# Turned sums ahead of a unit's own sums, and the last two node blocks side by side, in a two-layer graph network on one Trainium2 core

## The chip, the cores and the metric

One core of a Trainium2 chip runs the whole program. The metric is the device time of one execution in microseconds (us); several runs of the kernel before are given below. Five engines work side by side: PE multiplies matrices, DVE does elementwise vector work, ACT does activation functions and copies, POOL issues the gathers, SP issues most other transfers.

## The reference, cut to what matters

6250 nodes have 160 features each, 200000 edges join them and are sorted by their target node. Two layers follow each other; each sends messages over the edges, sums them by target, mixes the sums, adds the node's own part and normalises:

```
for layer in (0, 1):
    t   = per-node linear mix of x                    # the table that edges read
    w   = silu(edge_scalars @ fc1) @ fc2              # weights of an edge, 192 or 224
    msg = products of w, t[src] and 4 edge attributes # 448 or 640 wide
    agg = segment_sum(msg, dst)                       # by target node
    x   = layernorm(x + mix(agg) + own_mix(x))        # layer 1: silu and gates before the sum
```

Layer 1's table is made of layer 0's result, so no edge of layer 1 can be read before the last node of layer 0 is done.

## The kernel before, in words

Edges go in **tiles** of 128 (1563 of them), two tiles are a **pair** (782), four are a **unit** (391). Nodes go in **blocks** of 128 (49, named b0 to b48). Since edges are sorted, a run of 3 to 12 tiles touches at most 32 neighbouring nodes; such a run is a **group** (284 of them, named g0 to g283; n = 12 tiles at first, 4 tiles from about three quarters of the way on, 3 in the last fifth). `GROUPS`, `READY` (which group must be done before a block may be finished) and the tests on them are lines 37 to 68.

The loop of `windows` (lines 824 to 850) runs over units u, and each step works on several units at once:

- `gather` (line 703) for unit u+4: POOL issues one indirect DMA a tile. A gathered pair lies in one of 8 buffers `g`, so a gather waits for the products of 8 pairs earlier.
- `weights` (line 695, tile `pw`, 3 PSUM banks) for unit u+2 on PE: called W below.
- `hidden` (lines 646 to 677) for unit u+3: PE writes the two PSUM banks `pair0` and `pair1` (H below), ACT applies Silu out of them into `h`. In layer 0 one unit uses both banks, in layer 1 bank u % 2.
- `places` (line 734, tile `sel`) and `products` (line 721, tile `mid`) for the two pairs of unit u+2, all on DVE.
- `aggregate` (line 754, tile `pg`) for the four tiles of unit u on PE: A below. At a group's end ACT copies `pg` into `r` (and `rest` in layer 1).
- `turn` (lines 768 to 783) for the groups that ended in the unit before: PE transposes `r` into columns 256 and up of bank `pair[g % 2]` (T below), and DVE adds it into the sums `sm` and `sr` in SBUF (lines 781, 783), which hold all nodes.
- one step of the block that is being finished (`proceed`, line 816). In layer 0 these are `summed` (S below: PE multiplies `sm` and `sr`, DVE and ACT normalise), `turn` (line 520, n below: two transposes) and `mix` (m below: PE, then ACT writes the row to `table[1]`, the table that layer 1 gathers from). In layer 1 there is only `summed` (lines 558 to 582), which writes the output.
- one step of the own part of a block to come (`prepare`, line 796), in the middle of A: fetch, `self_part`, `self_mix`.

The order of PE's instructions is the order in which the program calls them: `matmul` and `transpose` (lines 137 to 145) pin it. DVE and ACT follow the order that the scheduler of the framework gives them, near the program's. All node work uses one PSUM bank, `pn` (bufs=1). PE's order in one unit of layer 0 is W, H, A, T, block step.

After the last unit, line 855 runs what is left of block steps one block after the other.

Of the kernel before, what the change touches and what calls it, by code (L numbers as in the profile page):

```python
# [16 lines left out]
P = 128  # L17
# [69 lines left out]
def kernel(ctx: ExitStack, tc: tile.TileContext, a, out):  # L87
# [345 lines left out]
    def turned(x, work, tag, bufs):  # L433

        n = x.shape[0]
        p = psum.tile([P, 512], F32, name=tag, bufs=bufs)
        transpose(p[:, 0:n], x[:, 0:P], ident[:n, :n])
        transpose(p[:V, P:P + n], x[:, P:D], ident[:n, :n])
        xt = work.tile([P, 2, P], F32, name="xt")
        nc.scalar.activation(xt[:, 0, :n], p[:, 0:n], AF.Copy)  # L440
        nc.scalar.activation(xt[:V, 1, :n], p[:V, P:P + n], AF.Copy)
        return xt
# [33 lines left out]
    def second_nodes(b, work, clear, name="nx"):  # L476


        n = rows_of(b)
        rows = slice(b * P, b * P + n)  # L480
        st = {}

        def fetch():
            x = st["x"] = work.tile([P, D], F32, name=name, bufs=4 if name == "nx" else 1)
            if b in owned:
                nc.sync.dma_start(x[:n], xown[rows, :])
            else:
                nc.sync.dma_start(x[:n], a["x_main"][:, b, :] if b < NB - 1 else a["x_tail"])

        def self_part():  # L490
            st["xs"] = turned(st["x"][:n], work, "pn", 1)

        def self_mix():
            x = st["x"]
            q = mixed(st["xs"], n, wsc, "pn", 1)
            for k in range(2):
                nc.vector.scalar_tensor_tensor(x[:n], q[:, k, :], own[:n, b, k:k + 1], x[:n],
                                               op0=OP.mult, op1=OP.add)
            return x

        def summed():
            p = psum.tile([P, 512], F32, name="pn", bufs=1)
            q = p[:n, :2 * D].rearrange("p (w d) -> p w d", w=2)
            for c in range(4):
                l = sm[:96, c, rows]
                if c < 2:
                    matmul(q[:, :, 0:S + V], l, rm0[:, c], start=(c == 0), stop=False)
                else:
                    v = S + (c - 1) * V
                    matmul(q[:, :, 0:S], l, rm0[:, c, :, 0:S], start=False, stop=False)  # L510
                    matmul(q[:, :, v:v + V], l, rm0[:, c, :, S:], start=False, stop=False)
            matmul(q[:, :, S + V:D], sr[:64, rows], rr0, start=False, stop=True)
            y = st["x"][:n]
            for k in range(2):
                nc.vector.scalar_tensor_tensor(y, q[:, k, :], gets[:n, b, k:k + 1], y,
                                               op0=OP.mult, op1=OP.add)
            mv = work.tile([P, 8], F32, name="mv")
            normed(y, mv)

        def turn():  # L520
            st["xt"] = turned(st["x"][:n], work, "pn", 1)

        def mix():
            xt = st["xt"]
            p = psum.tile([P, 512], F32, name="pn", bufs=1)
            matmul(p[:n, 0:P], xt[:, 0, :n], who[0][:, :P], start=True, stop=True)
            matmul(p[:n, P:D], xt[:V, 1, :n], who[1][:, :V], start=True, stop=True)
            r = work.tile([P, D], F32, name="nr")
            nc.scalar.activation(r[:n], p[:n, 0:D], AF.Copy, scale=nv[:n, b, 0:1])
            nc.scalar.dma_start(table[1][rows, :], r[:n])  # L530
            nc.scalar.dma_start(xmid[rows, :], st["x"][:n])
            if clear:
                nc.vector.memset(sm[:, :, b * P:b * P + P], 0.0)
                nc.vector.memset(sr[:, b * P:b * P + P], 0.0)

        return [fetch] + [self_part, self_mix] * (b not in owned), [summed, turn, mix]

    def last_nodes(b, work, clear):
        n = rows_of(b)
        rows = slice(b * P, b * P + n)  # L540
        st = {}

        def fetch():
            x = st["x"] = work.tile([P, D], F32, name="nx", bufs=4)
            nc.sync.dma_start(x[:n], xmid[rows, :])

        def self_part():
            st["xs"] = turned(st["x"][:n], work, "pn", 1)

        def self_mix():  # L550
            xt = st["xs"]
            p = psum.tile([P, 512], F32, name="pn", bufs=1)
            matmul(p[:n, 0:160], xt[:, 0, :n], who[0][:, P:], start=True, stop=True)
            matmul(p[:n, 160:192], xt[:V, 1, :n], who[1][:, V:], start=True, stop=True)
            o = st["o"] = work.tile([P, 192], F32, name="no", bufs=4)
            nc.scalar.activation(o[:n], p[:n, 0:192], AF.Copy)

        def summed():
            x, o = st["x"][:n], st["o"][:n]
            p = psum.tile([P, 512], F32, name="pn", bufs=1)  # L560
            q = p[:n, :192]
            matmul(q, sr[:, rows], rr1, start=True, stop=False)
            matmul(q[:, 0:160], sm[:, 0, rows], rm1[:, 0, 0:160], start=False, stop=False)
            for c in (1, 2, 3):
                v = slice(96 if c == 2 else 0, 192)
                matmul(q[:, v], sm[:, c, rows], rm1[:, c, v], start=False, stop=(c == 3))
            nc.vector.tensor_tensor(o, q, o, OP.add)
            f = nv[:n, b, 0:1]
            y = work.tile([P, D], F32, name="nr")
            nc.scalar.activation(y[:n, 0:S], o[:, 0:S], AF.Silu, scale=f)  # L570

            gate = work.tile([P, V], F32, name="gate")
            nc.scalar.activation(gate[:n], o[:, S:96], AF.Tanh, scale=half[:n, b])
            nc.vector.tensor_scalar(gate[:n], gate[:n], 1.0, half[:n, b], op0=OP.add, op1=OP.mult)
            nc.vector.tensor_tensor(
                y[:n, S:D].rearrange("p (c d) -> p c d", c=3),
                o[:, 96:192].rearrange("p (c d) -> p c d", c=3),
                gate[:n, None, :].to_broadcast([n, 3, V]), OP.mult)
            nc.vector.tensor_tensor(x, y[:n], x, OP.add)
            mv = work.tile([P, 8], F32, name="mv")  # L580
            normed(x, mv)
            nc.scalar.dma_start(out[rows, :], x)

        return [fetch, self_part, self_mix], [summed]


    def windows(i, loads, work, inputs_of):
# [208 lines left out]
        def prepare():  # L796

            if early:
                early.pop(0)()
            elif not coming and left and len(prepared) < 2:  # L800
                b = left.pop(0)
                if b in later:
                    later.remove(b)
                first_, then = nodes(b, work, i == 0)
                first_.pop(0)()
                coming.extend(first_)
                coming.append((b, then))
            elif len(coming) > 1:
                coming.pop(0)()
            elif later:  # L810
                early.extend(own_nodes(later.pop(0), work))
                early.pop(0)()
            if len(coming) == 1:
                prepared.append(coming.pop())
# [6 lines left out]
                going.pop(0)()  # L821
            return going or prepared

        for u in range(-4, units + 1):
            before = turned_to
            if i == 0 and ZERO + 4 + u < NB:
                zero(ZERO + 4 + u)
            if u + 4 < units:
                for p in pairs_of(u + 4):
                    gather(p)  # L830
            if 0 <= u + 2 < units:
                weights(pairs_of(u + 2))
            if 0 <= u + 3 < units:
                hidden(u + 3)
            if 0 <= u + 2 < units:
                for p in pairs_of(u + 2):
                    places(p)
                    products(p)
            if u >= 0:
                ended, waiting = waiting, []  # L840
                for t in range(4 * u, min(4 * u + 4, NT)):
                    if t == 4 * u + 2:
                        prepare()
                    aggregate(t)
                    if group_of[t][2]:
                        waiting.append(group_of[t][0])
                for g in ended:
                    turn(g)
                    turned_to = g + 1
                proceed(turned_to if u + 3 > units else before)  # L850
        for g in waiting:
            turn(g)
        while coming or left:
            prepare()
        while proceed(NG):
            pass


    def general(i, loads, work):
# [176 lines left out]
```

## Time and profile before

| what | us |
|---|---|
| runs of the kernel, median (lowest, highest) | 4095.0 (4084.81, 4096.76) |
| the profiled execution: its time, its span | 4098.12, 4096.3 |
| before the first gather | 65.8 |
| gathers of layer 0, first to last | 1989.0 |
| from the last gather of layer 0 to the first of layer 1 | 34.6 |
| gathers of layer 1, first to last | 1968.5 |
| after the last gather | 38.4 |
| busy: PE, DVE, POOL, ACT | 3522.1, 3095.1, 3026.7, 1176.1 |

A line of the timeline reads: start, duration, engine, line of the kernel, operation, written tile `<-` read tiles, shapes, how many such instructions were merged, and in brackets the idle time of the engine before it with what ended it. A line of the waits reads: engine, tile and line, what it waited for, us in total, how often, the longest. In the windows, each engine has its busy time and the number of its instructions, and PEclk is the granted clock of PE as a share of full speed. PE's records come two to a matmul.

### The profile page before, as it was taken

The numbers are of one execution on the slowest core, as the hardware profiler recorded it, in microseconds if no ns is written. First come the engines' busy times: TensorE is split into PE (matmuls) and PEld (weight loads), VectorE is DVE, ScalarE is ACT, GpSimd is POOL, SyncE is SP. The second block draws the span as 40 slices with busy tenths as digits, with TensorE's granted clock in tenths as the row PEclk, the third lists the DMA queues.
The fourth block names the chain that finished last, engine by engine and source line by source line (L and its number), as shares of the span: only waits on it lengthen the run. The fifth ranks groups of instructions, "written<-read, shape, count | busy, mean of one in ns | idle before, by whom it ended". The sixth has DMA issues, their size and how long they took to land. (4 is left out here: it accounts for less than half of the span.)

```text
span 4096.3 us, 108196 instructions
## 1 busy us (share of the span) xinstructions
PE 3522.1 (86%) x37363; PEld 2419.1 (59%) x37363; DVE 3095.1 (76%) x13202; ACT 1176.1 (29%) x4013; POOL 3026.7 (74%) x3232
## 2 busy tenths in 40 slices
PE   7788988889899999999978888888788888888887
PEld 5565666666666666666655555555555555555555
DVE  6676666667777777777757777777778888888887
ACT  2122221222222333333311111122223333444454
POOL 4777777777777777777757777777777777777774
PEclk8899898889899999999978888889989999998998
DMA  4233322222222232333323333333333333333332
GB/s 128 78 84 87 81 75 77 78 76 79 77 79 79 79 82 79 82 84 80 87 71 94 96 95 97 98 96 96 100 97 97 103 100 96 106 100 98 101 103 59
DMA packets 298517, 364.05 MB, mean 89 GB/s; under 512 B 86323, under 2 KB 246204, under 8 KB 297964
## 3 DMA queue, kind: packets, MB, share of 16 engines
q0 software_dynamic: 151056, 257.36, 23.8%
q1 hardware_dynamic: 121740, 85.59, 7.4%
q10 hardware_dynamic: 25168, 14.11, 1.1%
q8 instruction: 300, 4.92, 0.5%
q14 instruction: 253, 2.07, 0.2%
HBM read 338.73 MB, written 18.03 MB: 87 GB/s over the span
## 5 line engine op out<-in xcount | busy, mean ns | idle before, releaser
L703 POOL DMA_INDIRECT g<-table,src x3126 | 3004.9, 961 | 1026.8 <-issue 736.9
L721 DVE TENSOR_TENSOR mid<-g,pw 128x128 f32<-128x128 f32 (+2 forms) x7820 | 1852.8, 299 | 653.0 <-DMA g<-table,src 416.1
L138 PE MATMUL pw<-fc,h 100*128 100x192 f32 (+1 forms) x6252 | 1225.5, 383 | 193.4 <-DVE mid L721 186.4
L138 PE MATMUL pg<-mid,sel 128*32 128x160 f32 (+1 forms) x25008 | 1155.1, 305 | 0.0
L138 PEld LDWEIGHTS pw<-fc,h 100*128 100x128 f32 (+1 forms) x6252 | 895.9, 203 | 369.9 <-issue 315.0
L138 PEld LDWEIGHTS pg<-mid,sel 128*32 128x32 f32 x25008 | 755.3, 116 | 387.7 <-issue 320.7
L734 DVE SCALAR_TENSOR_TENSOR sel<-iota,off,ea 128x128 f32<-128x128 f32 x3126 | 940.5, 341 | 39.4 <-PE pg L138 35.0
L138 PE MATMUL pair<-e,fc 64*100 64x256 f32 (+1 forms) x2348 | 606.2, 454 | 120.2 <-DVE sr L783 113.4
L665 ACT ACTIVATE h<-pair 100x256 f32<-100x256 f32 x782 | 260.7, 381 | 954.6 <-PE pair L138 941.0
L138 PEld LDWEIGHTS pair<-e,fc 64*100 64x100 f32 (+1 forms) x2348 | 239.5, 183 | 351.2 <-issue 193.1
L676 ACT ACTIVATE h<-pair 128x256 f32<-128x256 f32 x392 | 150.5, 384 | 960.5 <-PE pair L138 795.6
L143 PE MATMUL pair<-ident,r 128*96 128x128 f32 (+1 forms) x852 | 225.7, 291 | 27.6 <-ACT h L665 21.7
L138 PE MATMUL pn<-rm,sm 96*128 96x128 f32 (+4 forms) x980 | 192.1, 356 | 51.2 <-DVE sm L781 49.6
L759 ACT ACTIVATE r<-pg 128x96 f32<-128x96 f32 (+1 forms) x568 | 149.5, 263 | 297.8 <-PE pg L138 228.5
L781 DVE TENSOR_TENSOR sm<-pair,sm 96x128 f32 (+1 forms) x568 | 161.9, 285 | 92.1 <-PE pair L143 19.1
L143 PEld LDWEIGHTS pair<-ident,r 128*96 128x96 f32 (+1 forms) x852 | 107.8, 127 | 206.0 <-issue 105.3
L765 ACT ACTIVATE rest<-pg 32x32 f32<-32x32 f32 x1136 | 209.5, 184 | 12.5
L138 PEld LDWEIGHTS pn<-rm,sm 96*128 96x128 f32 (+3 forms) x980 | 176.3, 235 | 59.9 <-DVE sm L781 53.3
L138 PE MATMUL pn<-rr,sr 64*128 64x128 f32 (+2 forms) x196 | 66.1, 426 | 93.4 <-DVE sr L783 89.0
L458 ACT ACT_TABLE_LOAD x97 | 124.5, 1283 | 7.1 <-DVE mv L457 5.4
L138 PEld LDWEIGHTS pair<-fold,rest 128*128 128x128 f32 x568 | 104.0, 226 | 1.1 <-ACT rest L765 1.1
L783 DVE TENSOR_TENSOR sr<-pair,sr 64x32 f32 (+1 forms) x568 | 99.7, 176 | 0.8 <-DVE sm L781 0.6
(137 smaller groups left out, 1313.0 us busy)
## 6 DMA issues: line engine op xcount, KB each, us to landing
g<-table,src POOLq DMA_INDIRECT x3126
e<-in_e SPq DMA_DIRECT2D x781, 64.0 KB
e<-in_e SPq DMA_DIRECT2D x390, 20.0 KB
ea<-in_ea_main SPq DMA_DIRECT2D x63, 96.0 KB
xg<-in_x_main SPq DMA_DIRECT2D x12, 320.0 KB
table<-rg SPq DMA_DIRECT2D x12, 320.0 KB
xmid<-nx ACTq DMA_DIRECT2D x48, 80.0 KB
table<-nr ACTq DMA_DIRECT2D x48, 80.0 KB
```

The source lines that it names most:

```text
L138: r = nc.tensor.matmul(*args, **kw)
L143: r = nc.tensor.transpose(*args)
L458: nc.scalar.activation(mv[:n, 1:2], mv[:n, 1:2], AF.Sqrt, bias=eps[:n])
L665: nc.scalar.activation(h[:100, 2 * P * j:2 * P * j + m], pair[j][:100, :m], AF.Silu)
L676: nc.scalar.activation(h[:kk, c0:c1], p[:kk, c0:c1], AF.Silu, scale=0.125)
L703: nc.gpsimd.indirect_dma_start(out=g[:n, j, :], out_offset=None, in_=table[i][:, :], in_offset=bass.IndirectOffsetOnAxis(ap=of(t)[0], axis=0))
L721: nc.vector.tensor_tensor(parts(mid[:n, :m], V * place, V * step, k), parts(g[:n, :m], c, V, k), parts(q[:n, :m], w, w_step, k), OP.mult)
L734: made["last"] = nc.vector.scalar_tensor_tensor(s[:n, j], iota[:n, None, :].to_broadcast([n, 4, W]), w, e[:, :, None].to_broadcast([n, 4, ...
L759: nc.scalar.activation(r[:, :w], pg[:, :w], AF.Copy)
L765: nc.scalar.activation(rest[g % 3][k, k], pg[k, P:P + V], AF.Copy)
L781: nc.vector.tensor_tensor(sm[:h, :, at], pt[:h, :P].rearrange("p (c w) -> p c w", c=4), sm[:h, :, at], OP.add)
L783: made["last"] = nc.vector.tensor_tensor(sr[:k, at], pt[:k, P:P + W], sr[:k, at], OP.add)
```

## The change

1. `turn` of the groups that ended in the unit before is called between the two pairs of `places` and `products`, that is ahead of `aggregate`. PE's order in a unit becomes W, H, T, A, block step; DVE's becomes first pair, adds, second pair.
2. The block b48 takes its PSUM tiles for node work from `pw` (3 banks) in place of `pn`, and in layer 0 its steps alternate with those of the block before it, after the last unit. The loop has one step less, and the last unit makes no block step.
3. `prepare` fetches a new block while fewer than three are prepared or in hand (four for the last one), in place of two prepared. By the rule of the loops, b48's own part in layer 1 comes at units 382 to 384 and not at 387 to 389; in layer 0 b47 and b48 are fetched at units 381 and 382 and not at 382 and 387.
4. In layer 1's last block an ACT instruction on one column calls Sqrt right after the gate's Tanh; the gate gets a tile of its own for input and output, and `mv` a ninth column for it.

```diff
+        bank = ("pn", 1) if b < NB - 1 else ("pw", 3)
...
-            p = psum.tile([P, 512], F32, name="pn", bufs=1)
+            p = psum.tile([P, 512], F32, name=bank[0], bufs=bank[1])
...
-            st["xt"] = turned(st["x"][:n], work, "pn", 1)
+            st["xt"] = turned(st["x"][:n], work, *bank)
...
+            if b == NB - 1:
+                nc.scalar.activation(mv[:n, 8:9], gates[:n, 0, 0:1], AF.Sqrt, bias=eps[:n], scale=0.0)
...
-            elif not coming and left and len(prepared) < 2:
+            elif not coming and left and len(prepared) + bool(going) < 3 + (left[0] == NB - 1):
...
-        for u in range(-4, units + 1):
+        for u in range(-4, units):
...
-            if 0 <= u + 2 < units:
-                for p in pairs_of(u + 2):
-                    places(p)
-                    products(p)
+            ps = pairs_of(u + 2) if 0 <= u + 2 < units else []
+            for p in ps[:1]:
+                places(p)
+                products(p)
+
+            ended, waiting = waiting, []
+            for g in ended:
+                turn(g)
+                turned_to = g + 1
+            for p in ps[1:]:
+                places(p)
+                products(p)
             if u >= 0:
-                ended, waiting = waiting, []
                 for t in range(4 * u, min(4 * u + 4, NT)):
                     if t == 4 * u + 2:
                         prepare()
                     aggregate(t)
                     if group_of[t][2]:
                         waiting.append(group_of[t][0])
-                for g in ended:
-                    turn(g)
-                    turned_to = g + 1
-                proceed(turned_to if u + 3 > units else before)
+                if u < units - 1:
+                    proceed(turned_to if u + 3 > units else before)
         for g in waiting:
             turn(g)
         while coming or left:
             prepare()
-        while proceed(NG):
-            pass
+
+        chains = [going] + [steps for _, steps in prepared]
+        while any(chains):
+            for steps in chains:
+                if steps:
+                    steps.pop(0)()
```

More of the change, by code (lines that the diff above doesn't have):

```diff
@@ L516, in summed @@
                                                op0=OP.mult, op1=OP.add)
-            mv = work.tile([P, 8], F32, name="mv")
+            mv = work.tile([P, 9], F32, name="mv")
             normed(y, mv)
         def turn():
-            st["xt"] = turned(st["x"][:n], work, "pn", 1)
+            st["xt"] = turned(st["x"][:n], work, *bank)
         def mix():
             xt = st["xt"]
-            p = psum.tile([P, 512], F32, name="pn", bufs=1)
+            p = psum.tile([P, 512], F32, name=bank[0], bufs=bank[1])
             matmul(p[:n, 0:P], xt[:, 0, :n], who[0][:, :P], start=True, stop=True)
@@ L570, in summed @@
             nc.scalar.activation(y[:n, 0:S], o[:, 0:S], AF.Silu, scale=f)
-            gate = work.tile([P, V], F32, name="gate")
-            nc.scalar.activation(gate[:n], o[:, S:96], AF.Tanh, scale=half[:n, b])
-            nc.vector.tensor_scalar(gate[:n], gate[:n], 1.0, half[:n, b], op0=OP.add, op1=OP.mult)
+            gates = work.tile([P, 2, V], F32, name="gate")
+            nc.scalar.activation(gates[:n, 0], o[:, S:96], AF.Tanh, scale=half[:n, b])
+            mv = work.tile([P, 9], F32, name="mv")
+            if b == NB - 1:
+                nc.scalar.activation(mv[:n, 8:9], gates[:n, 0, 0:1], AF.Sqrt, bias=eps[:n], scale=0.0)
+            gate = gates[:, 1]
+            nc.vector.tensor_scalar(gate[:n], gates[:n, 0], 1.0, half[:n, b], op0=OP.add,
+                                    op1=OP.mult)
             nc.vector.tensor_tensor(
@@ L579, in summed @@
             nc.vector.tensor_tensor(x, y[:n], x, OP.add)
-            mv = work.tile([P, 8], F32, name="mv")
             normed(x, mv)
```

## The prediction, before the result was known

> **What bounds the kernel now.** I read the page first, for the span (4096.3) and the costliest group, then POOL's waits.
>
> ```profile
> L703 POOL DMA_INDIRECT g<-table,src x3126 | 3004.9, 961 | 1026.8 <-issue 736.9
> ```
>
> ```profile
> POOL g L703 <- issue: 736.9, 2417, 0.3
> POOL g L703 <- DVE mid L721: 110.3, 361, 0.5
> ...
> POOL g L703 <- DMA nx<-xmid: 34.6, 1, 34.6
> ```
>
> POOL issues 3126 gathers of 961 ns, with 0.3 us between any two whatever is named as releaser; only one idle in the loops is longer, the 34.6 us between the layers. So in both layers POOL never stops, and the span is 65.8 + 1989.0 + 34.6 + 1968.5 + 38.4 = 4096.3. Next to nothing can be gained inside a layer. A gain must come out of the 34.6 and the 38.4, and a loss comes where another engine stops keeping POOL's pace.
>
> So I asked next who is nearest to that pace, by windows and in the timeline of late layer 0 (windows: PE, clock, DMA share, GB/s):
>
> ```profile
> 1746.00:1896.00 150.00, 140.09 (x1524) 0.95 0.30 80
> ```
>
> ```profile
> 1911.35 0.68 PE L138 MATMUL pair<-e,fc 64*100 64x256 f32 x4
> 1911.96 1.27 PE L138 MATMUL pg<-mid,sel 128*32 128x160 f32 x32
> ...
> 1918.49 1.75 PE L138 MATMUL pn<-rm,sm 96*128 96x192 f32 x12 [1.17 <-DVE sm L781]
> ...
> 1922.09 0.68 PE L138 MATMUL pair<-e,fc 64*100 64x256 f32 x4
> 1922.70 1.27 PE L138 MATMUL pg<-mid,sel 128*32 128x160 f32 x32
> 1924.70 0.85 PE L143 MATMUL pair<-ident,r 128*96 128x128 f32 x4 [0.73 <-ACT h L665]
> ```
>
> ACT in the same stretch:
>
> ```profile
> 1912.06 0.66 ACT L665 ACTIVATE h<-pair 100x256 f32<-100x256 f32 x2 [1.71 <-PE pair L138]
> ...
> 1922.70 1.28 ACT L665 ACT_TABLE_LOAD   x1
> 1923.99 0.66 ACT L665 ACTIVATE h<-pair 100x256 f32<-100x256 f32 x2
> ```
>
> PE is busy 140.1 of 150. From one start to the next, W takes 1.50, H 0.61, A 1.21, a T 0.39; a block's S takes 2.10, n 0.27, m 0.75. Late in layer 0 there is one block to four units and 5.33 groups, so four units cost PE 4 x 3.32 + 5.33 x 0.39 + 3.12 = 18.5, and with the waits shown (S for DVE's add 1.17, T for ACT's `h` 0.73) 20.4. POOL issued 118 gathers in those 150 us, 1.271 each: 20.3 for the sixteen of four units. PE has no slack there at all.
>
> **Part 1, T ahead of A, layer 0.** PE's last row shows a wait that matters more after the change: T starts 0.05 after ACT has finished with the bank that H wrote (h ends at 1924.65). T writes the same bank, so it can't pass Silu. Now A (1.21) lies between H and T and hides this. In front of A it is bare. By the rows of 1911: PE is free for T at 1911.96, `h` of the first bank ends at 1912.41 and of the second at 1912.72, so T waits 0.50 or 0.81, mean 0.65. After a summed block ACT first loads a table: at 1922.70 PE is free, T could start at 1924.37 or 1924.70, a wait of 1.85 in the mean. Four units now need 18.5 + 3 x 0.65 + 1.85 = 22.3, without the 1.17 and 0.73. PE becomes the bound by 2.0 in 20.3.
>
> How long: from unit 268 (its W at 1445) to the W of unit 388 (2060) PE has 120 units, all with a T: 120 x 3.32 + 143 turns x 0.39 + 25 blocks x 3.12 = 532, and the waits 95 x 0.65 + 25 x 1.85 = 108: 640 for the 615 now, **+25**. (Before unit 268 there are fewer turns and blocks, and PE stays under POOL's pace.) Queued behind the waiting T are A, the block step and the next W; DVE waits for T with its adds and, in order behind them, the second pair's products; these free the `g` buffers, and after about 13 us of lag POOL waits too.
>
> The clock comes on top. PE waited 1.47 at 1576.68, and the windows view gives 0.50 for 1578.3 to 1585.1: W took 2.93 in place of 1.50. Over the trace's clock records, 16 of 22 idle gaps of 1.8 to 2.0 us were followed by half clock, mostly for 3.4 or 6.8 us. The new 1.85 comes once a block: between 0 and 25 x 0.73 x 3.4 = 62. I take every second block at 2.8 of lost PE time, **+35**, a bit under the nearest rows, since in 6.8 us some of the time is waiting anyway.
>
> The Trainium skill ("TensorE: Matmul & The Clock Gate", "Why this matters for your kernels") sets the limit for dropping the clock at idle gaps of about 3 us between bursts. By it the clock would hold at 1.85 and the 35 would be 0; the rows at 1576 differ, and they decide.
>
> The other side of part 1: S no longer waits for the add, which DVE now does ahead of the second pair. In layer 0 this is in the 640.
>
> **Between the layers.**
>
> ```profile
> 2049.14 3.08 PE L138 MATMUL pn<-rm,sm 96*128 96x192 f32 x12 [3.16 <-DVE sm L781]
> ...
> 2076.47 3.11 PE L138 MATMUL pn<-rm,sm 96*106 96x192 f32 x12 [0.48 <-ACT nr L529]
> ```
>
> The first row is b46's S: 3.16 late, then at half speed (it is in the 615, not in the 640). The second is b48's S, waiting for `pn` until b47's mix has been copied, 7.7 after b47's S ended (2068.8). Side by side it needs b47's transposes (4.35 after S) and the adds of g282 and g283 (about 4.9 after): 2.8 earlier; the loop's end before it is about as long: **-3**, bounds 0 and -5. From there to the first gather of layer 1 at 2089.39 (12.9) the chain is as now. Layer 0 in sum: 25 + 35 - 3 = +57.
>
> **Layer 1 and the tail.** PE's four units there, by the timeline from 3925 to 3962 (each step from its start to the next): W 0.95, H 0.63, A 1.23, T with its gap 0.50, a block 2.83 (S 1.66, own part 0.37 and 0.80), T's wait about 0.45, since only half of the turns meet the bank of H: 17.6 of 20.1; PE stays free. DVE is near its limit:
>
> ```profile
> 4066.52 0.36 DVE L567 TENSOR_TENSOR no<-pn,no 128x192 f32<-128x192 f32 x1 [2.30 <-PE pn L138]
> ...
> 4074.24 0.90 DVE L721 TENSOR_TENSOR mid<-g,pw 64x64 f32<-64x64 f32 x6
> ```
>
> The last gather ends at 4057.89, its product starts at 4074.24: 16.35 behind, where 1.64 is the least in the trace and about 4 the mean two thirds through. DVE's cycle between two blocks is 20.3 (3934.90 to 3955.21), POOL's 20.1; in it `no` waits for PE's S, 63.0 us over 38 blocks, 1.66 each. With the adds ahead of the second pair (1.9 of DVE work, as long as S), that wait goes, DVE has 18.7 for 20.1, and the lag shrinks to about 6: **-10**, bounds 0 (what is saved is lost on T) and -14.7 (all lag). From the last product to b48's S (10.75 now) the chain of turns stays, so nothing more is counted.
>
> **The rest, each at 0.** The bank in layer 1: `pn` was read by 4080.33, b48's S started at 4084.99. The early Sqrt: the table load now runs from 4089.11 to 4090.39, hidden by DVE's steps up to 4090.60; the added call (0.29 by its sibling) lies beside DVE's gate. b48's own part leaves units 387 to 389: 1.3 of PE and 0.8 of ACT beside DVE's products, 0 to -1. The fetches on SP move one to five units forward, with four `nx` buffers; a wait of SP is covered by the three units that `e` is ahead. Moved parts issue the same DMAs as now.
>
> **Sum.** 57 - 10 = +47 on the profiled 4098.1 is 4145; the runs' median is 3.1 below that execution, so **4142**.
>
> **Rivals.** (B) PE is the bound but the clock holds: without the 35, +12, 4107. The 16 of 22 speak against it; that PE would be steadily loaded otherwise, for it. Range 4090 to 4120. (C) **Faster**: PE's bare T is absorbed. The buffers hold 13 us, and if T's mean wait is under about 0.4 (that is 18.5 + 1.6 = 20.1 for four units, POOL's pace) nothing of it reaches POOL. Then the end of layer 0 also loses the 3.16 and its half-speed units (S 1.3, W 1.4, H 0.5, A 1.1 longer than at full clock): -10 with the 2.8, and the tail gives -12: 4073. The rows of 1911 and 1922 speak against it; for it, that `h` could come sooner after H when ACT is idle. (D) DVE's order is the scheduler's, and the adds may stay behind the second pair: the change then doesn't do what it says on DVE, S waits as now, the tail's 10 is lost: 4152 or, on top of B, 4117. I count it into A and B.
>
> **Chances.** A (forecast) 0.50, 4115 to 4180; B 0.33; C 0.17. About 0.3% (12 us) can be told from no change. Slower by more (over 4107): A and half of B, 0.665; within: the other half of B and a little of C, 0.195; faster (under 4083): 0.14. The range 4078 to 4180 leaves out most of C and the top of A, under 0.2.
>
> **What would show it.** Right: POOL's waits for DVE mid grow late in layer 0 and its 1989.0 becomes some 2030 or more; `PE L143 <- ACT h L665` grows from 21.7 to over 150; PEclk late in layer 0 falls under 0.95; `no <- PE pn` nearly goes and the 38.4 falls to about 28. Wrong: the gathers of layer 0 still take 1989 with T waiting (C), or the wait of T is not there at all.

## The result and the profile after

The changed kernel takes 4184.02 us in the median of four runs (4172.53 to 4191.97), the kernel before 4093.91 on the same chip. The ratio is 1.0227, interval 1.0205 to 1.0248: **slower by 90 us, where the forecast was 47**, and 4 us above the forecast's range. The profiled execution took 4183.07 us, span 4181.3.

| part of the span, us | before | after | difference | forecast |
|---|---|---|---|---|
| before the first gather | 65.8 | 66.0 | +0.2 | 0 |
| gathers of layer 0 | 1989.0 | 2075.3 | +86.3 | +60 |
| last gather of layer 0 to first of layer 1 | 34.6 | 45.6 | +11.0 | -3 |
| gathers of layer 1 | 1968.5 | 1962.6 | -5.9 | 0 |
| after the last gather | 38.4 | 31.8 | -6.6 | -10 |

In the kernel after, a line that was 721 is 728, 665 is 672, 734 is 741, 781 is 788, 783 is 790, 567 is 569; 143 and 460 are as before. The costliest group and two of POOL's waits, where POOL never stopped inside a layer before:

```profile
L710 POOL DMA_INDIRECT g<-table,src x3126 | 2999.3, 959 | 1124.0 <-issue 740.2
```

```profile
POOL g L710 <- DVE mid L728: 178.8, 336, 5.0
POOL g L710 <- DMA nx<-xmid: 45.6, 1, 45.6
```

The gathers themselves are as short as before (959 ns for 961), so the time that was added stands in the idle column: 1124.0 us for 1026.8, 97 more. POOL's idle times are no longer 0.3 us each: a wait for the products has 5.0 us for its longest, where 0.5 was the longest before. Now the window that the forecast showed of before (140.09 us of PE's 150, the clock at 0.95), taken of after. The columns are the window, its length, the busy times of PE, PE's weight loads, DVE, ACT and POOL with the number of their instructions, then the clock, the DMA share and the GB/s:

```profile
1746.00:1896.00 150.00, 122.11 (x1235) 88.20 (x1234) 95.70 (x403) 47.71 (x145) 97.67 (x101) 0.91 0.26 70
```

Every engine is less busy than before (PE 122 us for 140, DVE 96 for 116, ACT 48 for 54), and POOL issues 101 gathers for 118. A learner who looks for the busiest engine finds none. PE is nevertheless what ends last, and its waits say why:

```profile
PE pair L143 <- ACT h L672: 225.6, 254, 3.8
...
PE pair L143 <- ACT h L683: 152.9, 189, 3.1
PE pn L143 <- DVE nx L460: 43.0, 28, 4.6
```

The first row is T in layer 0, and was 21.7 us in 22 waits; the second is T in layer 1. One unit, as the timeline has it, first PE and then ACT (a transpose has one record, so T's x2 is one group and its x4 are two):

```profile
1987.16 0.68 PE L138 MATMUL pair<-e,fc 64*100 64x256 f32 x4
1988.58 0.46 PE L143 MATMUL pair<-ident,r 128*96 128x128 f32 x2 [0.74 <-ACT h L672]
1988.97 1.27 PE L138 MATMUL pg<-mid,sel 128*32 128x160 f32 x32
1990.17 1.57 PE L138 MATMUL pw<-fc,h 100*128 100x192 f32 x8
```

```profile
1987.87 0.66 ACT L672 ACTIVATE h<-pair 100x256 f32<-100x256 f32 x2 [1.71 <-PE pair L138]
```

H ends, ACT reads its bank until 1988.53, T starts at 1988.58. A needs nothing of this and stands in the queue behind it. The costlier form comes behind a summed block:

```profile
1998.01 0.68 PE L138 MATMUL pair<-e,fc 64*100 64x256 f32 x4
2002.45 1.20 PE L143 MATMUL pair<-ident,r 128*96 128x128 f32 x4 [3.77 <-ACT h L672]
```

```profile
1998.71 0.38 ACT L672 ACTIVATE h<-pair 100x256 f32<-100x256 f32 x1 [3.75 <-PE pair L138]
1999.12 1.28 ACT L458 ACT_TABLE_LOAD   x1
2000.41 0.29 ACT L458 ACTIVATE mv<-mv,eps 128x1 f32<-128x1 f32 x1
2000.72 1.28 ACT L672 ACT_TABLE_LOAD   x1
...
2002.02 0.38 ACT L672 ACTIVATE h<-pair 100x256 f32<-100x256 f32 x1
```

ACT's order has put the block's square root, with both its table loads, between the two Silu of one unit, so T waits 3.77 and not the forecast's 1.85. The two groups' T behind it lasts 1.20, where such a T took 0.85 at 1924.70 in before: it lies in a clock record of 0.5, from 2001.2 to 2008.0. In the 119 units from the W of unit 270 to that of 389 this happens in 14 (in none before), and 8 of T's waits there are of this length.

**The account of that stretch.** I split PE's time by step; a step's time runs from its start to the next step's, less the idle time shown in brackets. The half clock's part is half of PE's busy time inside the clock records at 0.5, taking the work there to last twice as long (W took 2.93 at 1579.09, for 1.57).

| us, PE, 119 units | before | after |
|---|---|---|
| work at full clock | 527.8 | 529.9 |
| lost to half clock | 34.3 | 40.7 |
| T waits | 10.3 | 108.4 |
| S waits for the adds | 34.3 | 0.0 |
| n waits for DVE's normalised rows | 0.3 | 14.4 |
| all (before with H's 0.8) | 607.9 | 693.3 |

The same work takes PE 85.4 us longer, nearly all of it waiting: T waits 98 us more and n 14, S waits 34 less, and half clock takes 6 more. In before, PE's 45 us of waits were time that POOL needed anyway.

### The profile page after: what moved, and what is told of

Read it like the earlier page. It is cut to its first block, busy times and chain, and to the rows that moved or that the text cites. A ratio compares the mean times of both kernels' runs of the same rounds, so it can differ in the third digit from the quotient of the medians.

```text
span 4181.3 us, 108231 instructions
## 1 busy us (share of the span) xinstructions
PE 3460.6 (83%) x37363; PEld 2370.1 (57%) x37363; DVE 3087.7 (74%) x13202; ACT 1181.1 (28%) x4014; POOL 3020.9 (72%) x3232
## 5 line engine op out<-in xcount | busy, mean ns | idle before, releaser
L710 POOL DMA_INDIRECT g<-table,src x3126 | 2999.3, 959 | 1124.0 <-issue 740.2
L138 PE MATMUL pw<-fc,h 100*128 100x192 f32 (+1 forms) x6252 | 1213.9, 383 | 192.4 <-DVE mid L728 184.1
L138 PE MATMUL pg<-mid,sel 128*32 128x160 f32 (+1 forms) x25008 | 1151.4, 304 | 0.0
L138 PEld LDWEIGHTS pw<-fc,h 100*128 100x128 f32 (+1 forms) x6252 | 884.0, 203 | 450.8 <-issue 385.1
L138 PEld LDWEIGHTS pg<-mid,sel 128*32 128x32 f32 x25008 | 748.5, 116 | 211.4 <-issue 124.4
L138 PE MATMUL pair<-e,fc 64*100 64x256 f32 (+1 forms) x2348 | 577.6, 443 | 19.1 <-DVE sr L790 12.9
L143 PE MATMUL pair<-ident,r 128*96 128x128 f32 (+1 forms) x852 | 228.2, 293 | 379.6 <-ACT h L672 225.6
L143 PEld LDWEIGHTS pair<-ident,r 128*96 128x96 f32 (+1 forms) x852 | 108.7, 128 | 612.9 <-ACT h L672 337.4
L138 PEld LDWEIGHTS pair<-e,fc 64*100 64x100 f32 (+1 forms) x2348 | 231.2, 179 | 237.1 <-issue 202.0
L138 PE MATMUL pn<-rm,sm 96*128 96x128 f32 (+3 forms) x968 | 152.1, 305 | 0.4 <-DVE sm L788 0.4
L138 PEld LDWEIGHTS pn<-rm,sm 96*128 96x128 f32 (+2 forms) x968 | 138.8, 194 | 13.1 <-issue 10.5
L138 PEld LDWEIGHTS pair<-fold,rest 128*128 128x128 f32 x568 | 107.8, 234 | 9.9 <-ACT rest L772 3.6
L790 DVE TENSOR_TENSOR sr<-pair,sr 64x32 f32 (+1 forms) x568 | 100.0, 176 | 2.0 <-issue 1.0
L143 PE MATMUL pn<-ident,nx 128*128 128x128 f32 (+1 forms) x242 | 63.2, 351 | 44.4 <-DVE nx L460 43.0
```

Of the source, the lines that this page charges most:

```text
L138: r = nc.tensor.matmul(*args, **kw)
L143: r = nc.tensor.transpose(*args)
L710: nc.gpsimd.indirect_dma_start(out=g[:n, j, :], out_offset=None, in_=table[i][:, :], in_offset=bass.IndirectOffsetOnAxis(ap=of(t)[0], axis=0))
L790: made["last"] = nc.vector.tensor_tensor(sr[:k, at], pt[:k, P:P + W], sr[:k, at], OP.add)
```

## The experiments

My theory, M: T waits bare for ACT's Silu on the bank that H has just written, this makes PE the bound of late layer 0, and nothing else in the change costs anything. Rivals: R1, the loss comes from the order of DVE's adds; R2, from the clock, which differs by itself; R3, from the side-by-side blocks, the own parts or the early square root.

| kernel | what it is | ratio to before (interval) | layer 0, gap, layer 1, tail (us) | T waits late in layer 0 (us) |
|---|---|---|---|---|
| after | the change | 1.0227 (1.0205 to 1.0248) | 2075.3, 45.6, 1962.6, 31.8 | 108.4 |
| E1 | before, T moved only | 1.0288 (1.0263 to 1.0312) | 2083.4, 49.5, 1964.8, 35.9 | 108.2 |
| E2 | after, T put back | 0.9993 (0.9979 to 1.0007) | 1983.2, 31.6, 1964.8, 32.9 | 11.7 |
| E3 | after, T ahead in layer 1 only | 0.9999 (0.9987 to 1.0012) | 1986.7, 35.0, 1964.4, 35.2 | 9.8 |
| E4 | after, T ahead of H | 1.0029 (1.0017 to 1.0042) | 1994.4, 36.2, 1969.9, 36.4 | 0.0 |
| E5 | after, T in the middle of A | 0.9986 (0.9975 to 0.9997) | 1981.1, 31.5, 1965.0, 28.1 | 27.0 |
| E5 again | the same kernel | 0.9987 (0.9977 to 0.9998) | 1991.1, 36.3, 1967.5, 26.8 | 25.7 |
| E6 | after, T in a bank of its own | 1.0081 (1.0055 to 1.0107) | 1988.3, 28.5, 1993.6, 38.3 | 14.2 |
| E7 | after, two banks for W | 1.0391 (1.0374 to 1.0409) | 2038.3, 39.2, 2058.2, 41.2 | 94.7 |
| E8 | E7, PE busy in T's wait | 1.0437 (1.0419 to 1.0454) | 2054.3, 40.0, 2061.3, 42.2 | 60.4 |
| E9 | after, T ahead until unit 267 | 1.0035 (1.0021 to 1.0049) | 1996.0, 32.6, 1963.5, 34.3 | 13.0 |
| E10 | after, T ahead from unit 268 | 1.0178 (1.0156 to 1.0199) | 2052.8, 45.6, 1964.6, 36.4 | 108.7 |
| E11 | after, both Silu together | 1.0230 (1.0210 to 1.0250) | 2065.3, 47.6, 1962.3, 35.0 | 114.7 |

The last column goes from the W of unit 270 to that of unit 389 and leaves out waits under 0.2 us. The two profiled executions of E5 differ by 10 us in layer 0 and by 5 in the gap. So of the fourth column I read no difference below that; small ones are read from the ratios.

### E1 and E2: the move alone, and all but the move

E1, against before (E2 is the same edit backwards, against after):

```diff
...
-                for p in pairs_of(u + 2):
-                    places(p)
-                    products(p)
...
+            for p in ps[:1]:
+                places(p)
+                products(p)
...
+            for g in ended:
+                turn(g)
...
+            for p in ps[1:]:
+                places(p)
+                products(p)
             if u >= 0:
...
                 for t in range(4 * u, min(4 * u + 4, NT)):
...
-                for g in ended:
-                    turn(g)
...
```

> The kernel before with one thing changed: the turn T of a pair stands ahead of its unit's aggregate A in layers 0 and 1 (W, H, T, A for W, H, A, T). Theory M (T then waits bare for ACT's Silu over the bank of the hidden values, about 0.65 us a time, and PE becomes the bound of late layer 0): 4175 to 4195 us, the gathers of layer 0 take 2070 to 2080 us for 1989.0, and the wait of T for ACT's h of layer 0 grows from 21.7 us to over 180. R1 (the order of VectorE's adds carries the loss): within 15 us of the kernel before, 4094. R3 (the side-by-side last blocks, the own parts ahead or the earlier square root carry it): within 15 us of 4094 too.

> The kernel after with T put back behind A in both layers, all else kept. Theory M: the loss goes, 4080 to 4095 us, the gathers of layer 0 take 1985 to 1995 us, T's waits for ACT's h fall to some 20 us, and the tail behind the last gather keeps its gain (34 to 38 us for 38.4). R1 and R3: the loss stays, 4165 to 4190 us. R2 (the granted clock differs by itself between executions): no order among the two kernels of this job, both off by tens of us with no change in T's waits.

E1 4204.04 us, E2 4084.27, before 4087.84. The move alone has the whole loss, T's late waits to 0.2 us the same as in after; without it nothing is lost. E1 is even 0.6% above after (1.0288 for 1.0227, the intervals apart), on another chip: whether the other parts save something where T stands ahead was not separated. T's group in E2, to be set beside after's idle time of 379.6 us, and its costliest group:

```profile
L143 PE MATMUL pair<-ident,r 128*96 128x128 f32 (+1 forms) x852 | 226.2, 291 | 35.2 <-ACT h L672 25.1
```

```profile
L710 POOL DMA_INDIRECT g<-table,src x3126 | 2995.3, 958 | 1025.5 <-issue 731.1
```

T's work is the same (226.2 us), only its idle time is gone, and POOL's idle time is back at the 0.3 us between gathers. R3 falls as the cause of the loss: where T stands behind A, parts 2 to 4 of the change are worth -0.0007, no change that can be told. R2 falls as well: on one chip all ten runs of E2 (4076 to 4099 us) lie below all four of E1 (4199 to 4212), and the order goes with T's waits.

### E3: T ahead in layer 1 only

```diff
-            for g in ended:
+            for g in ended if i == 1 else []:
                 turn(g)
...
+                for g in ended if i == 0 else []:
+                    turn(g)
+                    turned_to = g + 1
```

> The kernel after with T ahead of A in layer 1 alone, behind A in layer 0. Theory M with PE the bound of late layer 0 only: the waits for ACT's h stay in layer 1 (some 150 us) and go in layer 0, and the time is 4075 to 4095 us with the gathers of layer 1 at 1960 to 1968 us, since POOL sets layer 1's pace. Rival (every bare wait of T costs its length wherever it stands): layer 1's gathers take 2040 us or more, 4150 us or more.

4091.55 us, 0.9999, layer 1's gathers 1964.4. The wait is there and costs nothing:

```profile
PE pair L143 <- ACT h L683: 151.1, 188, 3.1
```

So 151 us of bare waits are free in layer 1, where PE has slack, and 108 us of the same kind in late layer 0 cost some 76 (E10 below), S's 34 us of waits being saved in return. The total of a wait is no price.

### E5, E6 and E4: is it the bank, or the place?

E5 leaves T in a shared bank and covers its wait by half of A; E6 gives T a bank of its own and leaves it ahead of A; E4 lets it pass in front of H.

E5:

```diff
-            for g in ended:
-                turn(g)
-                turned_to = g + 1
...
                     if t == 4 * u + 2:
                         prepare()
+                        for g in ended:
+                            turn(g)
+                            turned_to = g + 1
                     aggregate(t)
```

E6 (the banks of W wherever they are named):

```diff
-            pt = pair[g % 2][:, 2 * P:]
+            pt = psum.tile([P, 512], F32, name="pt", bufs=1)
...
-                pw = psum.tile([P, 512], F32, name="pw", bufs=3)
+                pw = psum.tile([P, 512], F32, name="pw", bufs=2)
```

E4:

```diff
+            ended, waiting = waiting, []
+            for g in ended:
+                turn(g)
+                turned_to = g + 1
             if 0 <= u + 3 < units:
                 hidden(u + 3)
...
-            ended, waiting = waiting, []
-            for g in ended:
-                turn(g)
-                turned_to = g + 1
```

> The kernel after with T in the middle of A, behind two of the unit's four tiles. The half of A (some 0.7 us of PE's time) is as long as the wait that T had for ACT's Silu (0.74 us, 225.6 us in all of layer 0). Theory M: T's waits for ACT's h of layer 0 fall under 50 us, the gathers of layer 0 take 1985 to 2000 us, the time is 4080 to 4100 us. Rival (T's place ahead of the sums costs by itself, whatever it waits for, since it holds A back by T's own work of some 0.7 us): half of the loss stays, 4120 to 4150 us.

> The kernel after, T ahead of A as there, but with a PSUM bank of its own for the turned sums (the weights W get two banks in place of three for it, so this run carries that change too). Theory M: T has nothing to wait for, its waits for ACT's h of layer 0 go from 225.6 us to under 20, and the gathers of layer 0 take 1985 to 2010 us unless the third bank of W is missed (then W waits for VectorE's products, and that wait shows by name); 4080 to 4110 us. Rival (place, not bank): T's waits go and the loss stays, 4150 to 4190 us with PE busy all through late layer 0.

> The kernel after with T ahead of H instead (W, T, H, A), so that T finds its bank free and H has to wait until VectorE has added T's sums out of the bank. Theory M by its mechanism (the bank shared by H and T is the resource): the wait does not go but changes its name, T's waits for ACT's h under 20 us, H's waits for VectorE's sr over 100 us in layer 0, the gathers of layer 0 take 2030 to 2080 us, 4120 to 4190 us. Rival (only the wait for ACT's Silu counts): 4065 to 4095 us.

**E5** 4083.93 us: some 0.7 us of cover take T's waits in late layer 0 from 108 to 27 us, and the loss is gone. In all of layer 0 its row, 225.6 us in after, is

```profile
PE pair L143 <- ACT h L672: 54.4, 38, 3.2
```

**E6** has T ahead of A and DVE's adds between the pairs just as after has them, and layer 0 is back at 1988.3 us. So neither the place nor DVE's order costs anything there (R1 falls), the shared bank does. How much of the 87 us goes with T's bank is read against E7, which has two banks for W as E6 has and T in the shared bank: its layer 0 is 2038.3, so T's own bank is worth 50 us, and the other 37 go with the two banks of W, for a reason that stays open. E6's total is 4119.91, above what I expected, for layer 1 has become longer by 29 to 31: the missing third bank, taken up in E7. **E4** shows the bank from the other side. T waits for nothing, H waits instead:

```profile
PE pair L138 <- DVE sr L790: 343.1, 357, 3.8
```

This is the wait that M expected, but it cost less than M expected (4101.29 us, 1.0029): in the late stretch H waits 60.9 us and T none, where T waited 108.4 in after. By its price E4 lies between M's range and the rival's.

### E9 and E10: before and behind unit 268

The forecast took the units before 268 as free. E9's condition is below; E10's is `u >= 268`.

```diff
-            for g in ended:
+            for g in ended if i == 1 or u < 268 else []:
                 turn(g)
...
+                for g in ended if not (i == 1 or u < 268) else []:
+                    turn(g)
+                    turned_to = g + 1
```

> The kernel after with T ahead of A in layer 0 only up to unit 267 (and in layer 1), behind A from unit 268 on. The after lost 12 us by unit 270. If PE can't make that up later, since it has no slack there, layer 0's gathers take 1996 to 2008 us, 4090 to 4105 us in all. Rival (the later stretch makes it up out of the 46 us that PE waits there in the order before): 1984 to 1994 us, 4075 to 4095 us in all.

> The kernel after with T ahead of A in layer 0 only from unit 268 on. If the stretches add up, layer 0's gathers take 2055 to 2070 us, 4155 to 4175 us in all. Rival (the early delay is made up by the buffers, so that the late stretch carries the whole): 2070 to 2080 us, 4170 to 4190 us in all. The forecast's own sum for this stretch was 57, which would be 2046 us.

E9 4100.37 us, E10 4165.19, before 4085.52 on this chip. Set against E2's 0.9993 the early units cost 0.0042 of the time, about 17 us, the late ones 0.0185, 76 us; together 93, and after itself stands 0.0234, 96 us, above E2. The two stretches add up. W of unit 270 starts at 1457 to 1463 us in the kernels with three banks for W and T ahead there (after, E1, E9, E11) and at 1439 to 1445 in those with T behind or halfway (before, E2, E3, E5, E10). Between units 150 and 270 T waits 73.7 us in after, for 7.9 in before; that PE stays under POOL's pace there only on the average would explain the delay, but no run shows where it arises. E7 and E8 have T ahead too, and start that W at 1449.9 and 1443.6 with 67 and 38 us of T's waits there, so the waits alone don't set it.

### E7 and E8: two banks for W, and PE kept busy in the wait

E7 has the second half of E6's edit alone. E8 is E7 with this on top, `junk` being a PSUM bank of its own that nothing reads:

```diff
             if i == 0:
+                for _ in range(2):
+                    transpose(junk[:, :P], ident, ident)
                 transpose(pt[:96, :P], r[:, :96], ident)
```

> The kernel after with two PSUM banks for the weights W in place of three, nothing else: the control for the run in which T had its own bank. If the 26.6 us by which layer 1's gathers were longer there come from the missing third bank, they come here too: layer 1's gathers 1985 to 2000 us, layer 0 still long at 2070 to 2100, 4200 to 4230 us in all. Rival (T's own bank made layer 1 slow): layer 1's gathers 1962 to 1970 us, 4180 to 4195 in all.

> The control with two transposes of a constant (some 0.55 us) put ahead of each T of layer 0, into a bank that nothing reads: PE has work that nobody needs while it would wait for ACT's Silu, so the length of the wait stays and its idleness goes. The output is as before. If the half clock that follows idle PE costs what the forecast said (35 us), layer 0's gathers get 20 to 45 us shorter than the control's and the time at half clock in late layer 0 falls from some 89 us to under 50. Rival (half clock falls into time that waits anyway): layer 0 within 8 us of the control, or longer where the two transposes last longer than the wait.

E7 4248.38 us. Layer 1's gathers take 2058.2, so the missing bank makes layer 1 long without T's own bank, and the rival falls. It costs more here (E6 has 1993.6), where T is in the shared bank as well. Layer 0 is shorter than in after, 2038.3 for 2075.3, which neither side expected. By the account T waits 14 us less and the half clock takes 17.4 in place of 40.7 in the late stretch; only 4 of T's waits last over 3 us, for 8. Why ACT's order meets T's bank less often there stays open.

E8 4266.74 us. T's waits in layer 0, E7's row and then E8's (where 143 is 144 and 672 is 673):

```profile
PE pair L143 <- ACT h L672: 197.3, 255, 3.8
```

```profile
PE pair L144 <- ACT h L673: 116.4, 217, 3.5
```

The transposes (some 60 us in the late stretch) fill most of the short waits: of 0.4 to 1 us E7 has 111 there, E8 12. But 10 waits of over 3 us are left, for E7's 4, and the half clock lasts 64.9 us for 41.0. My expectation of a shorter layer 0 fell. Short idle times are not what halves the clock here, and the clock records say the same: in E7, with 111 of them, seven stretches of half clock begin in the late stretch, six of them within 4 us of the start of a wait of T of 1.8 us or more, the seventh behind a wait of 0.53 and one of 1.21. What the half clock costs by itself can't be read from E8, since more of the long waits are left.

### E11: both Silu of a unit together

ACT's Silu of layer 0 and the square roots are held to the program's order, which takes all 21 splits away.

```diff
-        nc.scalar.activation(mv[:n, 1:2], mv[:n, 1:2], AF.Sqrt, bias=eps[:n])
+        r = nc.scalar.activation(mv[:n, 1:2], mv[:n, 1:2], AF.Sqrt, bias=eps[:n])
+        if pinned[0]:
+            tc.keep_in_program_order(r)
...
-                    nc.scalar.activation(h[:100, 2 * P * j:2 * P * j + m], pair[j][:100, :m], AF.Silu)
+                    tc.keep_in_program_order(nc.scalar.activation(
+                        h[:100, 2 * P * j:2 * P * j + m], pair[j][:100, :m], AF.Silu))
```

> The kernel after with ACT's order held to the order of the program for layer 0's Silu and the square roots, so that no square root stands between the two Silu of a unit (21 units in the after, 14 of them late). If the waits of 3.5 to 4 us (30 of the 108 us of T's waits between units 270 and 389) and the half clock behind them are part of the loss, T waits 85 to 98 us there, half clock falls from 88.7 to under 65, layer 0's gathers take 2040 to 2062 us, 4145 to 4170 us in all. Rival (the time behind a table load is waited for in any order): T's waits within 5 us of 108, 4175 to 4195 us.

4186.05 us, 1.0230: as after. The rival was right. T's waits in layer 0 (line 674 was 672):

```profile
PE pair L143 <- ACT h L674: 234.6, 253, 4.5
```

In the late stretch the 8 waits of 3.8 us become 20 of 2.2, T's waits go from 108.4 to 114.7, and n's from 14.4 to 0.0, with the square root ahead of both Silu. So the time of the table loads is waited for in both orders, in long waits of T and n or in more of T's. The stretch is 13 us shorter and W of unit 270 stands 6 us later; nothing of it shows in the median.

### E5 again

> The kernel with T in the middle of A once more, to tell its small gain from none (it was 0.9986 of the kernel before): 4080 to 4090 us, ratio 0.997 to 1.0. If the gain was chance, the interval takes in 1.

4091.69 us for 4095.24, 0.9987. Both intervals end below 1. E5 is the one version here that is faster than before, by some 0.13% (5 us), and it is 2.4% faster than after.

### The first chip

The first four runs, E1 to E4, fell on another chip, on which the kernel before took 6033.2 us, 1.47 times as long, at granted clocks of about 0.75. Their expectations were made for the usual times and don't apply.

> The kernel before with nothing changed but the place of the turned sums: PE's order is W, H, T, A, block step, DVE's is first pair, adds, second pair. Theory M (T waits bare for ACT's Silu on the bank that H wrote, and PE is the bound of layer 0 from about unit 210 on): the gathers of layer 0 take 2070 to 2080 us as in the changed kernel, T's waits for h in units 268 to 387 sum to about 108, the gap between the layers stays near 46 to 50, the tail is 30 to 34; time 4175 to 4195. Rival R3 (the side-by-side blocks, the own parts further ahead and the early Sqrt carry the loss): layer 0 near 1990, time 4080 to 4110.

> The changed kernel with the turned sums back behind the unit's own sums; the second bank, the side-by-side blocks, the own parts ahead and the early Sqrt stay. Theory M: the gathers of layer 0 take 1985 to 1995, the gap between the layers 30 to 33, the tail 36 to 38; time 4085 to 4095, within 0.3% of before. Rival R3: 4150 or more.

> The changed kernel with the turned sums ahead in layer 1 alone; in layer 0 they stay behind the unit's own sums. Theory M: layer 0 as before (1989, gap 31), layer 1 and its tail as in the changed kernel (tail 31 to 33, gathers 1963 to 1968); time 4078 to 4088, 6 to 16 faster than before. Rival R1 (the loss is DVE's order, adds between two pairs, which frees the gather buffers later, in whichever layer): layer 1 loses as much as layer 0 did and the time is above 4100.

> The changed kernel with the turned sums one step further ahead, between W and H: PE's order is W, T, H, A, block step, so T meets a bank whose Silu is a unit old; DVE makes the adds ahead of both pairs. Theory M: T waits for h nearly never, layer 0 takes 1985 to 2000, S doesn't wait for the adds, the gap is near 25 and the tail 28 to 33; time 4065 to 4085. H may wait for DVE's adds instead, which would show as PE pair L138 <- DVE sr. Rival R1 (the loss comes from early adds on DVE that keep the second pair's products back): layer 0 stays above 2040. Rival R2 (any early turn breaks up PE's work and drops the clock): PEclk late in layer 0 stays at 0.94 or under and layer 0 above 2020.

E1 took 5799.47 us (0.9623, interval 0.9593 to 0.9652), E2 5989.90 (0.9934, 0.9907 to 0.9960), E3 5876.65 (0.9739, 0.9714 to 0.9765), E4 6160.85 (1.0216, 1.0189 to 1.0243). The order is turned round: T ahead of A is faster there. E2's POOL waits on that chip:

```profile
POOL g L710 <- DVE mid L728: 1849.4, 491, 10.3
```

In E2's other run it is 114.9 us, at about the same busy time of DVE (3088 us, and 3062 on the first chip). So POOL is far from the bound there. H waits long for DVE's adds (`PE pair L138 <- DVE sr L790` has 358.0 us with a longest of 7.8), and it may be that adds that come earlier are worth more than T's wait costs; that was not tried by itself. PE is busy for 4539 us, 3508 in the other run, and its clock record is at 0.5 for 2937 us of 5984. Why the chip is like this I can't say; what it shows is that the sign of such a move is not a property of the move alone.

## Why the prediction was right in kind and short by half

**Right: the wait, its place and its length.** T waits bare for ACT's Silu, in late layer 0, and E1, E2, E5, and E6 set against E7, show that this is the cause. The forecast's 108 us of T's waits is 108.4. Its parts were off in opposite directions: 106 waits of under 1 us hold 68.9 where 62 were forecast; behind a block there are 4 of 1.8 us, one of 2.1 and 8 of 3.8, 39.6 us for 46.

**Right: the work and, nearly, the clock as a total.** The base of 532 for 120 units is 527.6 for 119, measured 529.9 at full clock. The 35 for half clock is 40.7, and in E11, where no late wait of T is longer than 2.5 us, it is 35.9. As an addition to before the 35 is wrong: before had already lost 34.3 to half clock in this stretch, behind the waits of S, so the change adds 6.4. The 615 of before holds that loss and the 640 set against it doesn't, so nearly all of the +35 belongs to the +25: measured, the waits add 77 (T 98 and n 14 more, S 34 less). The sum of the two is what can be compared, not the split. Half clock came 12 times at 25 blocks, "every second block" as forecast, but that is in part luck: it was put on 25 waits of 1.85, and 10 of the 12 stand behind the 13 long waits of T that there were, two behind waits of n that the forecast didn't have. The Trainium skill ("TensorE: Matmul & The Clock Gate", "Why this matters for your kernels") has some 3 us for the idle gap that drops the clock, by which E11's would have been 0; the measurement decides.

**Failed step 1, the late stretch's sum.** "120 x 3.32 + 143 turns x 0.39 + 25 blocks x 3.12 = 532, and the waits ... 108: 640", with 35 for the clock, is 669 for 119 units; measured 693.3. The missing 24 are n's wait, 14.4, which the forecast didn't have, the clock's 6, and 4 of work and T. I had asked what S gains by the earlier adds (it waits 34.3 us less), and not what is late next: n, behind S on PE, waits for rows whose square root ACT's new order puts behind a Silu. E11, with the root ahead of both Silu, has 0.0 there.

**Failed step 2, the early units.** "Before unit 268 there are fewer turns and blocks, and PE stays under POOL's pace" was argued from the average. E9 puts 17 us on these units. By unit 270 after is 12 us later than before, and the four kernels named at E9 are in the mean 19 us later than those with T behind. E9's late stretch is 8 us shorter than that of before (599.7 us for 607.9), so part of the delay is made up where PE may go faster than POOL; in after, where PE is the bound, it adds to the rest.

**Failed step 3, the end.** The forecast's -10 of the tail was worked out from DVE's wait for S, and that wait went as it said, 63.0 us to this:

```profile
DVE no L569 <- PE pn L138: 13.4, 14, 2.3
```

But the lag didn't shrink to 6: the last product starts 12.6 us behind the last gather, for 16.35. (The least lag in the trace of before is 1.60 and not 1.64, which moves only a bound.) The step that fails is "that wait goes, DVE has 18.7 for 20.1": `no` waits less, and DVE waits elsewhere. Late in layer 1 (3700 to 4145 us, in before 3600 to 4050) its products wait 12.5 us for W, 4.8 in before, and its adds 24, 13 in before. Nor does the tail follow the adds. The kernels with T ahead of A in layer 1 and three banks for W (after, E1, E3, E9, E10, E11) have tails of 31.8 to 36.4 us and lags of 12.6 to 17.0, one profiled execution each, and `no` waits 12 to 15 us in all of them; E2 and E5, where `no` waits 56 to 66 us, have tails of 32.9, 28.1 and 26.8 and lags of 11.6, 8.7 and 6.5. So no run ties the -6.6 of after to the forecast's reason, and what shortens the tail was not separated.

**Between the layers** the forecast had -3. E2, where layer 0 isn't late, has 31.6 for 34.6; E3 and E5's second execution show 35.0 and 36.3, so this can't be told from none. In after b48's S starts right behind b47's transposes, as forecast (2173.42, where the transposes started at 2172.97), but PE enters the gap with the products some 20 us behind the gathers (3 to 4 before), and the gap grows by 11. I had counted this lag as part of layer 0's end and not of the gap; it is the same time, and the table's two rows go together: +97 for the forecast's 57.

**Rivals.** B (the clock holds) fell by the 40.7. C (absorbed) is what happens in layer 1, and E3 shows it; in layer 0 PE has no room. D fell, the adds do stand between the pairs (at 1989.13 and 1989.34 in after, between products that start at 1986.61 and 1989.43). Of the 38 us by which the two profiled executions miss the sum (85 for 47), 26 lie in the late stretch, 12 in the early units and 3 each in the gap and the tail, less the 6 by which layer 1's gathers were shorter.

## What to carry to other kernels

Before an instruction is moved forward in an in-order queue, look at what it shares with its new neighbour: here T stood 0.05 us behind ACT's last read of the PSUM bank of H, though it writes other columns of it, and everything behind T waited too. (Whether the chip or the framework's order holds it back, no run separates.) A wait costs nothing where its engine has slack and most of its length where it has none (108 us of T's waits cost 76 here), so ask for each stage which engine ends last, not how long the wait is in all. If an early place is wanted, half of an independent step in front of it may be enough cover, as it was in E5.

## What the runs showed of the hardware

- **A bound engine may look idle.** In after, PE is busy 122 us of 150 in the stretch that it bounds, less than before (140), where POOL bounded it.
- **Half clock came behind waits of PE of over 1 us, and not behind shorter ones alone.** In after, twelve stretches of half clock begin late in layer 0: ten within 4.6 us of the start of a wait of T of 1.8 to 3.8 us, two behind a wait of 0.53 and one of 1.21, and none behind one of the 106 waits of T under 1 us alone. In E11, with no wait of T over 2.5 us, PE ran 75 us at half clock there, and each of its 17 stretches of it stands behind a wait of 1.66 to 2.49 us; in E8, with nearly all short waits filled and 10 over 3 us left, 65; in E6, with 14 us of T's waits, none over 1 us, 20.
- **One chip took 1.47 times as long for the same program**, with DVE, ACT and POOL busy for about the same time (in E2 3062, 1182 and 3062 us for 3088, 1176 and 3017), PE for 4539 us in place of 3508 at a granted clock of 0.755 in place of 0.901, and waits of POOL for DVE of up to 10.3 us; and it turned the order of the versions round (E1 0.9623 for 1.0288, E4 1.0216 for 1.0029).
